# States on the partitions: a selective scan laid out by 4 states x 32 channels, its sum over the states made in four column quarters of TensorE

## The chip, the cores and the metric

The kernel runs on one core of one Trainium2 chip. The time is the device time of one execution in microseconds, as the median of several runs. Beside it there is one profiled execution, with a record of every instruction of the five engines: TensorE (PE, with its weight loads PEld), VectorE (DVE), ScalarE (ACT), GpSimd (POOL) and SyncE (SP), which here only issues DMAs.

## The reference, cut to what matters

One decoder layer on `x[8, 256, 256]` (batch, time, width) in f32: a Mamba block, a cross attention with a feed-forward, and a mixture of 160 experts. The change is in the Mamba block (512 channels, 16 states):

```python
u = silu(conv4(x @ in_x) + conv_b)                  # [256 t, 512 channels]
dt, Bm, Cm = split(u @ x_proj, [16, 16, 16])        # Bm, Cm: [256 t, 16 states]
delta = softplus(dt @ dt_proj + dt_b)               # [256 t, 512]
A = -exp(A_log)                                     # [512, 16]
for t in range(256):                                # per channel d and state n
    h[d, n] = h[d, n] * exp(delta[t, d] * A[d, n]) + delta[t, d] * u[t, d] * Bm[t, n]
    y[t, d] = sum_n h[d, n] * Cm[t, n]
y = (y + u * D_param) * silu(x @ in_z)
x = layernorm(x + y @ out_proj)
```

Then `x = layernorm(...)` of the attention block on `ctx`, with a feed-forward of 1024, and `x = layernorm(x + moe(x))` with the 8 best of 160 experts per token. The 8 batch rows are independent up to the experts.

## The kernel before, in words

**Stages.** The first stage does Mamba, attention and routing for one batch row after another (0 to some 855 us), then what is left of the last row (to some 950), then the expert blocks to the end. The change touches the first stage.

**A step.** The scan of a row is 16 steps, one for each state. Partitions are 128 channels, and the free side holds 4 channel groups x 256 times, so a step is one tile of 128 x 1024. In step n

- GpSimd makes `g = du * B[n]` (`product`, L348),
- ScalarE makes the four decays `exp(delta * A)` into PSUM (`decays`, L353),
- VectorE runs two scans of 512 columns into the PSUM tile `states` (`scans`, L363) and reads them out times `C[n]` into `h` (`read_out`, L372),
- TensorE adds `h` into the row's sum `ya` with two products against the identity (`summed`, L381); at state 0 it also adds `D_param * u` by a diagonal matrix (L384).

The rows `B[n]` and `C[n]` are the same for all channels, so they are loaded from DRAM to all partitions, four states in one DMA of 512 KB (`bc_load`, L340).

**What runs beside the steps.** Three Python generators are advanced by `go()` between the parts of a step: `head(b + 1)` makes the next row's u, z, B, C and delta (convolution L279, SiLU, Exp, L324, Ln, the subtraction on GpSimd L329, L332, `du` L334); `rest(b - 1)` does the row before: gate (L400), output projection (L406), layernorm, attention (scores' maximum L466, values L494), feed-forward (L524, L535, L540), layernorms and router (probabilities L567, the best eight L577, their sum L584, its reciprocal L592, places L602); `scatter` (L628) writes the routing table by indirect DMAs on GpSimd.

**What sets the order.** For PE, ACT, DVE and POOL the whole stage lies in one `manual_schedule`: each engine runs its instructions in the order in which the program text emits them, so the order is the sequence of `go()` calls in the loop over the 128 steps. The products run `LEAD` = 3 steps ahead of the scans:

```python
scans(b, n, made)
while ahead < min(i + LEAD + 1, len(steps)) and "du" in rows_made[steps[ahead][0]]:
    product(*steps[ahead], rows_made[steps[ahead][0]])
    ahead += 1
```

The SP queue, which issues the DMAs, is ordered by a scheduler. Two PSUM banks turn for everything but the held tiles (`decay`, `states`) and `ya`.

Of the kernel before, what the change touches and what calls it, by code (L numbers as in the profile page):

```python
# [29 lines left out]
NG = 4  # L30
# [17 lines left out]
C_BQ = C_ALOG + KI * NS  # L48
# [14 lines left out]
def decoder_layer(  # L63
# [109 lines left out]
    with ExitStack() as first:  # L173
# [3 lines left out]
        m3 = first.enter_context(tc.tile_pool(name="m3", bufs=3))  # L177
        m4 = first.enter_context(tc.tile_pool(name="m4", bufs=4))
        pools["ps"] = first.enter_context(tc.tile_pool(name="ps_front", bufs=2, space=PSUM))
# [3 lines left out]
        a2 = first.enter_context(tc.tile_pool(name="a2", bufs=2))  # L183
# [6 lines left out]

        def load_x(b):
            xt = m2.tile([P, KD, S], F32, tag="xt", name=f"xt_{b}")
            nc.sync.dma_start(xt, x_t[:, b, :].rearrange("(k p) t -> p k t", p=P))
            return xt
# [3 lines left out]
        xt0 = load_x(0)  # L198
        in_sb = weight(in_w, KD, 2 * DI, "in_sb")
# [10 lines left out]
        none = wts.tile([P, D], F32, name="none")  # L210
# [17 lines left out]
        na = wts.tile([P, KI * NS], F32, name="na")  # L228
        exps()
        nc.scalar.activation(na, cv[:, C_ALOG : C_ALOG + KI * NS], AF.Exp)  # L230
# [6 lines left out]


        decay = [held.tile([P, 2, S], F32, name=f"decay{j}") for j in range(KI // 2)]
        for t in decay:  # L240
            nc.vector.memset(t[:, :, 0:1], 0.0)
        states = held.tile([P, KI, S], F32, name="states")
        states_f = states.rearrange("p k t -> p (k t)")
# [5 lines left out]
        def head(b, xt, made):  # L249

            u = m2.tile([P, KI, S], F32, tag="u", name=f"u_{b}")
            sz = m2.tile([P, KI, S], F32, tag="sz", name=f"sz_{b}")

            def projected(j):

                pj = bank(f"pj_{b}_{j}").rearrange("p (e t) -> p e t", e=2)
                for e in range(2):
                    o = (2 * j + e) * P
                    for k in range(KD):
                        nc.tensor.matmul(  # L260
                            pj[:, e, :], in_sb[:, k, o : o + P], xt[:, k, :], start=(k == 0), stop=(k == KD - 1)
                        )
                return pj

            for j in range(KI // 2):
                pj = projected(j)
                yield
                for e in range(2):
                    k = 2 * j + e
                    nc.scalar.activation(  # L270
                        u[:, k, :], pj[:, e, :], AF.Identity, bias=cv[:, C_CONVB + k : C_CONVB + k + 1],
                        scale=cv[:, C_CONVW + (k + 1) * NTAP - 1 : C_CONVW + (k + 1) * NTAP],
                    )
                yield
                for e in range(2):
                    k = 2 * j + e
                    for i in range(NTAP - 1):
                        late = NTAP - 1 - i
                        nc.vector.scalar_tensor_tensor(  # L279
                            u[:, k, late:], pj[:, e, : S - late],  # L280
                            cv[:, C_CONVW + k * NTAP + i : C_CONVW + k * NTAP + i + 1], u[:, k, late:], ALU.mult, ALU.add,
                        )
                    if e == 0:
                        yield
            for j in range(KI // 2):
                pz = projected(KI // 2 + j)
                yield
                nc.scalar.copy(sz[:, 2 * j : 2 * j + 2, :], pz)
            nc.scalar.activation(u, u, AF.Silu)
# [6 lines left out]
            xd = m2.tile([RK + 2 * NS, S], F32, tag="xd", name=f"xd_{b}")  # L296
            nc.scalar.copy(xd, px[: RK + 2 * NS, :S])
            bc_d = dr.tile([2, NS, S], F32, tag="bc_d", name=f"bc_d_{b}")
            nc.sync.dma_start(bc_d.rearrange("a n t -> (a n) t"), xd[RK:, :])
            made["bc_d"] = bc_d  # L300
# [5 lines left out]
            delta = m2.tile([P, KI, S], F32, tag="delta", name=f"delta_{b}")  # L306
# [26 lines left out]
            du = m2.tile([P, KI, S], F32, tag="du", name=f"du_{b}")  # L333
            nc.gpsimd.tensor_mul(du, delta, u)  # L334
            made.update(u=u, sz=sz, delta=delta, du=du)

        def bc_load(b, i, n, bc_d):

            t = m2.tile([P, NG, S], F32, tag=f"bc{i}", name=f"bc{i}_{b}_{n}")
            nc.sync.dma_start(t, bc_d[i, n : n + NG, :].partition_broadcast(P))  # L340
            return t

        def product(b, n, made):

            if n % NG == 0:
                made["b_rows"] = bc_load(b, 0, n, made["bc_d"])
            g = m4.tile([P, KI, S], F32, tag="g", name=f"g_{b}_{n}")
            nc.gpsimd.tensor_mul(g, made["du"], mid(made["b_rows"][:, n % NG, :], KI))  # L348
            made[n] = g.rearrange("p k t -> p (k t)")

        def decays(b, n, made):
            for k in range(KI):
                nc.scalar.activation(  # L353
                    decay[k // 2][:, k % 2, 1:], made["delta"][:, k, 1:], AF.Exp,
                    scale=na[:, k * NS + n : k * NS + n + 1],
                )

        def scans(b, n, made):

            gf = made.pop(n)  # L360
            for j in range(KI // 2):
                part = slice(j * NT, (j + 1) * NT)
                nc.vector.tensor_tensor_scan(  # L363
                    states_f[:, part], decay[j].rearrange("p k t -> p (k t)"), gf[:, part], 0.0, ALU.mult, ALU.add
                )

        def read_out(b, n, made):

            if n % NG == 0:
                made["c_rows"] = bc_load(b, 1, n, made["bc_d"])  # L370
            h = m3.tile([P, KI, S], F32, tag="h", name=f"h_{b}_{n}")
            nc.vector.tensor_mul(h, states, mid(made["c_rows"][:, n % NG, :], KI))  # L372
            made["h"] = h.rearrange("p k t -> p (k t)")

        def summed(b, n, made, hf):

            if n == 0:
                made["ya"] = [acc.tile([P, NT], F32, tag="acc", name=f"ya_{b}_{j}") for j in range(KI // 2)]
            ya, u = made["ya"], made["u"]
            for j in range(KI // 2):  # L380
                nc.tensor.matmul(ya[j], ident, hf[:, j * NT : (j + 1) * NT], start=(n == 0), stop=(n == NS - 1))  # L381
            if n == 0:
                for k in range(KI):
                    nc.tensor.matmul(  # L384
                        ya[k // 2][:, (k % 2) * S : (k % 2 + 1) * S], diag[:, k, :], u[:, k, :],
                        start=False, stop=False,
                    )

        def rest(b, sz, ya):

            xn = a2.tile([P, TT, D], F32, tag="xn", name=f"xn_{b}")
            nc.sync.dma_start(xn, x[b].rearrange("(c p) d -> p c d", p=P))
            ct = a2.tile([P, KD, S], F32, tag="ct", name=f"ct_{b}")
            nc.sync.dma_start(ct, cx_t[:, b, :].rearrange("(k p) t -> p k t", p=P))
            cn = a2.tile([P, TT, D], F32, tag="cn", name=f"cn_{b}")
            nc.sync.dma_start(cn, cx[b].rearrange("(c p) d -> p c d", p=P))

# [24 lines left out]
            def biased(pp, bias, name):  # L422
                dst = a1.tile([P, KD, S], F32, tag=name, name=f"{name}_{b}")
# [7 lines left out]
            kt = biased(pk, C_BK, "kt")  # L431
            x1 = a2.tile([P, TT, D], F32, tag="x1", name=f"x1_{b}")
            layernorm(x1, xn, f"x1_{b}")
            yield
            val = a1.tile([P, TT, D], F32, tag="val", name=f"val_{b}")
# [14 lines left out]
            qt = biased(pq, C_BQ, "qt")  # L450
# [18 lines left out]
            prob = a1.tile([P, TT, S], F32, tag="prob", name=f"prob_{b}")  # L469
# [176 lines left out]
        with tc.manual_schedule(engines={E_.PE, E_.Activation, E_.DVE, E_.Pool}):  # L646
            for _ in head(0, xt0, rows_made[0]):
# [12 lines left out]
            steps = [(b, n) for b in range(B) for n in range(NS)]  # L660
            ahead = 0
            for i, (b, n) in enumerate(steps):
                made = rows_made[b]
                if n == 0:
                    if b + 1 < B:
                        heads.append(head(b + 1, load_x(b + 1), rows_made[b + 1]))
                    if b == 0:
                        product(0, 0, made)
                        ahead = 1
                        decays(0, 0, made)  # L670
                if n == NS - 2:
                    while heads:
                        go(heads)
                scans(b, n, made)
                while ahead < min(i + LEAD + 1, len(steps)) and "du" in rows_made[steps[ahead][0]]:
# [4 lines left out]
                go(rests)  # L680

                if i > 0:
                    b0, n0 = steps[i - 1]
                    summed(b0, n0, rows_made[b0], rows_made[b0]["h"])
                if n % 2 == 0:
                    go(heads)
                read_out(b, n, made)
                if n == 0 and b > 0:
                    before = rows_made[b - 1]
                    rests.append(rest(b - 1, before["sz"], before["ya"]))  # L690
                    next(rests[-1])
                else:
                    go(rests)
                go(heads)
                go(scattered)
                if len(rests) > 1:
                    go(rests)
                if len(rests) > 1 and n > 0:
                    go(rests)
# [6 lines left out]
            summed(B - 1, NS - 1, made, made["h"])  # L706
# [239 lines left out]
def laid_out(inputs):  # L946
# [5 lines left out]
    def columns(v, width=1):  # L952
# [13 lines left out]
        "in_w": get(a + "in_proj_w").T,  # L966
# [13 lines left out]
                columns(get(a + "A_log"), NS),  # L980
# [34 lines left out]
```

## Time and profile before

| | before |
|---|---|
| median of 3 runs | 1525.78 us (1523.56 to 1527.69) |
| profiled execution, its own time | 1523.81 us |
| its span | 1522.1 us |
| mean granted TensorE clock | 0.872 |
| busy: PE / PEld | 1125.7 / 747.6 us |
| busy: DVE / ACT / POOL | 875.8 / 667.5 / 882.7 us |
| scan stage, first scan to the end of the last row's steps | 44 to some 855 us |

How to read it: busy time is a sum over the whole span, and the stages differ. In the scan stage all four compute engines are busy by turns, in the expert stage (950 to 1522 us) GpSimd and TensorE are. PEld is the loading of weights into TensorE, which runs beside its products. An f32 product is recorded as two passes. A number in brackets behind an instruction is the idle time of its engine ahead of it, and the arrow names what ended it.

### The profile page before, as it was taken

What the parts mean: (1) busy time and instruction counts of PE and PEld (TensorE: products, weight loads), DVE (VectorE), ACT (ScalarE), POOL (GpSimd) and SP (SyncE); (2) the same over time, 40 slices, a digit from 0 to 9 for tenths busy, and PEclk for the clock granted to TensorE, in tenths of its full rate; (3) what the DMA queues carried; (4) which work ended last, traced back from release to release, by engine and by line L of the source; (5) the groups of instructions that cost most, each with busy time, mean ns of one, the idle gap of its engine ahead of it and who ended that gap; (6) DMA issues with size and microseconds to landing.
All of it is one profiled execution on the core that took longest, in us unless ns stands there. A gap on an engine that the chain in (4) does not pass through costs nothing. (4 is left out here: it accounts for less than half of the span.)

```text
span 1522.1 us, 16364 instructions
## 1 busy us (share of the span) xinstructions
PE 1125.7 (74%) x4319; PEld 747.6 (49%) x4319; DVE 875.8 (58%) x1773; ACT 667.5 (44%) x1540; POOL 882.7 (58%) x713
## 2 busy tenths in 40 slices
PE   4567688787888878877788661088888888868675
PEld 3324455455455545554455441065666666644333
DVE  2789679669777787787688218189333333310000
ACT  4375654845855757648545331022222222212222
POOL 1664365664756756847676015565666666637775
PEclk8779998889989989989889775589999999986877
DMA  8212812121212313134211000077867778634443
GB/s 274 72 47 87 295 34 67 46 62 50 50 49 57 44 47 77 42 55 44 62 29 14 21 7 8 7 226 206 245 189 215 218 228 249 191 107 134 132 135 90
DMA packets 110294, 160.20 MB, mean 105 GB/s; under 512 B 20756, under 2 KB 77622, under 8 KB 110192
## 3 DMA queue, kind: packets, MB, share of 16 engines
q1 hardware_dynamic: 77680, 114.50, 27.1%
q0 software_dynamic: 20704, 33.81, 8.3%
q10 hardware_dynamic: 11808, 10.75, 2.0%
q8 instruction: 38, 0.62, 0.2%
q14 instruction: 64, 0.52, 0.2%
HBM read 152.15 MB, written 43.58 MB: 129 GB/s over the span
## 5 line engine op out<-in xcount | busy, mean ns | idle before, releaser
L348 POOL TENSOR_TENSOR g<-du,bc 128x1024 f32<-128x1024 f32 x128 | 299.9, 2354 | 87.4 <-DVE states L363 69.9
L363 DVE TENSOR_TENSOR_SCAN states<-decay,g 128x512 f32<-128x512 f32 x256 | 314.6, 1229 | 58.7 <-ACT decay L353 25.9
L353 ACT ACTIVATE decay<-delta,na 128x255 f32<-128x255 f32 x512 | 238.0, 474 | 130.1 <-DVE states L363 119.2
L830 POOL DMA_INDIRECT xg<-x_d,tokens x216 | 216.0, 1000 | 131.6 <-PE bt L841 121.9
L381 PE MATMUL ya<-h,ident 128*128 128x512 f32 x512 | 264.0, 648 | 29.9 <-DVE h L372 29.9
L843 DVE COPY bx<-bt 128x256 f32<-128x256 f32 x216 | 91.5, 424 | 180.6 <-PE bt L841 179.6
L852 PE MATMUL by<-we,bg 128*128 128x256 f32 x432 | 151.3, 432 | 44.5 <-ACT bg L850 36.8
L381 PEld LDWEIGHTS ya<-h,ident 128*128 128x128 f32 x512 | 102.3, 208 | 135.2 <-issue 78.7
L850 ACT ACTIVATE bg<-bh 128x128 f32<-128x128 f32 x216 | 59.8, 277 | 247.7 <-PE bh L846 243.2
L372 DVE TENSOR_TENSOR h<-states,bc 128x1024 f32<-128x1024 f32 x128 | 156.2, 1220 | 7.9
L628 POOL DMA_INDIRECT tab_d<-pair_no,placei x128 | 130.7, 1021 | 42.0 <-issue 30.0
L934 POOL DMA_INDIRECT y<-y_d,sloti x128 | 121.0, 945 | 58.4 <-issue 35.3
L940 PE MATMUL yn<-y,diags 128*128 128x256 f32 x256 | 110.8, 551 | 42.4 <-DMA y<-y_d,sloti 41.3
L846 PEld LDWEIGHTS bh<-bx,we 128*128 128x128 f32 x864 | 130.0, 193 | 20.2 <-DVE bx L843 8.2
L846 PE MATMUL bh<-bx,we 128*128 128x128 f32 x864 | 134.7, 279 | 4.1 <-DVE bx L843 2.8
L852 PEld LDWEIGHTS by<-we,bg 128*128 128x128 f32 x432 | 65.2, 189 | 96.7 <-ACT bg L850 96.2
L940 PEld LDWEIGHTS yn<-y,diags 128*128 128x128 f32 x256 | 56.2, 257 | 94.8 <-DMA y<-y_d,sloti 90.0
L941 DVE TENSOR_TENSOR xs<-xs,yn 128x512 f32<-128x512 f32 x8 | 5.5, 688 | 158.1 <-PE yn L940 158.1
L524 PE MATMUL ph<-x2t,w_sb 128*128 128x256 f32 x256 | 71.9, 443 | 31.6 <-ACT x2t L512 31.2
L841 PE MATMUL bt<-ident,xg 128*128 128x128 f32 x432 | 83.5, 275 | 3.8 <-DMA xg<-x_d,tokens 3.8
L524 PEld LDWEIGHTS ph<-x2t,w_sb 128*128 128x128 f32 x256 | 56.3, 225 | 51.3 <-ACT x2t L512 37.0
L260 PE MATMUL pj<-xt,in_sb 128*128 128x256 f32 x256 | 65.7, 403 | 17.6 <-DMA in_sb<-in_in_w_dram 8.3
(220 smaller groups left out, 1609.9 us busy)
## 6 DMA issues: line engine op xcount, KB each, us to landing
we<-in_experts_dram SPq DMA_DIRECT2D x216, 256.0 KB, 3.4
bc<-bc_d SPq DMA_DIRECT2D x64, 512.0 KB, 5.7
y_d<-bo SPq DMA_DIRECT2D x216, 128.0 KB, 3.0
y_d<-none ACTq DMA_DIRECT2D x1, 9216.0 KB, 31.4
xg<-x_d,tokens POOLq DMA_INDIRECT x216, 3.6
xt<-in_x_t_dram SPq DMA_DIRECT2D x8, 256.0 KB
w_sb<-in_w_dram SPq DMA_DIRECT2D x2, 1024.0 KB, 10.9
xn<-in_x_dram SPq DMA_DIRECT2D x8, 256.0 KB, 5.2
```

Of the source, the lines that this page charges most:

```text
L348: nc.gpsimd.tensor_mul(g, made["du"], mid(made["b_rows"][:, n % NG, :], KI))
L353: nc.scalar.activation(decay[k // 2][:, k % 2, 1:], made["delta"][:, k, 1:], AF.Exp, scale=na[:, k * NS + n : k * NS + n + 1],)
L363: nc.vector.tensor_tensor_scan(states_f[:, part], decay[j].rearrange("p k t -> p (k t)"), gf[:, part], 0.0, ALU.mult, ALU.add)
L372: nc.vector.tensor_mul(h, states, mid(made["c_rows"][:, n % NG, :], KI))
L381: nc.tensor.matmul(ya[j], ident, hf[:, j * NT : (j + 1) * NT], start=(n == 0), stop=(n == NS - 1))
L524: nc.tensor.matmul(ph[:, i, :], w1_sb[:, k, f * P : (f + 1) * P], x2t[:, k, :], start=(k == 0), stop=(k == KD - 1),)
L628: nc.gpsimd.indirect_dma_start(out=tab_views[i * TOPK + j], out_offset=bass.IndirectOffsetOnAxis(ap=placei[:, c, j : j + 1], axis=0), in_= ...
L830: nc.gpsimd.indirect_dma_start(out=xg[i % LANES], out_offset=None, in_=x3_d, in_offset=bass.IndirectOffsetOnAxis(ap=tokens[:, i : i + 1], ...
L846: nc.tensor.matmul(ph, w[:, k * P : (k + 1) * P], xt[:, k * P : (k + 1) * P], start=(k == 0), stop=(k == KD - 1))
L852: nc.tensor.matmul(py, g, w[:, KD * P :], start=True, stop=True)
L934: nc.gpsimd.indirect_dma_start(out=y8[:, j, :], out_offset=None, in_=y_d, in_offset=bass.IndirectOffsetOnAxis(ap=sloti[:, i, j : j + 1], a ...
L940: nc.tensor.matmul(pn[:, c, :], diags[:, i, j, :], y8[:, j, :], start=False, stop=(j == TOPK - 1))
```

## The change

A step is now 32 channels with all 16 states, in place of one state with all 512 channels. The partitions are 4 states x 32 channels, the free side 4 groups of states x 256 times. There are still 16 steps to a row (`NC` = 16 channel groups), with a tile of 128 x 1024 in each, and the product, the four decays, the two scans and the read-out keep their number, shapes and engines.

- **The sum over the states** now runs over the partitions too. A matrix `over` of 128 x 32 adds the four states of each channel. Every four steps, `summed` makes 16 products of 256 columns, each into 32 partitions of `ya`: the four steps of a group go to the four quarters of the partitions, named by `tile_position`. The part `D_param * u` goes first (`skipped`, at step 2).
- **B and C** of a row are loaded once, into two tiles of 128 x 1024 (`rows_of`: eight DMAs of 128 KB, each to 32 partitions).
- **delta and delta * u** need each channel on four partitions. Both are stored to DRAM at the end of a head (`spread_d`, 512 KB each) and loaded back for two steps at a time (`spread`: eight DMAs of 64 KB), up to four pairs ahead (`PAIRS`).
- **The order**: heads start at step 2 of a row in place of step 0, advance twice a step in place of one and a half times, and are flushed at step 10 in place of 14. `rest` gets one more stage ahead of the gate, and its later stages are reached at other points of the steps.
- **Buffers**: `in_w` comes as two halves; `xt`, `u`, `v`, `delta`, `xd` and the tiles of `rest` have one buffer; kt, qt, values and probabilities share one tile (`early`) with `ht`; `none` shares one with `pr`; `h` has five buffers; the spread tiles have four.

```diff
-NG = 4
+NR = 4
+NG = NS // NR
+CH = P // NR
+NC = DI // CH
+NP = NC // 2
+PAIRS = 4
 LEAD = 3
...
+        over = wts.tile([P, CH], F32, name="over")
+        nc.vector.tensor_add(over, ident[:, :CH], ident[:, CH : 2 * CH])
+        for r in range(2, NR):
+            nc.vector.tensor_add(over, over, ident[:, r * CH : (r + 1) * CH])
...
-            du = m2.tile([P, KI, S], F32, tag="du", name=f"du_{b}")
-            nc.gpsimd.tensor_mul(du, delta, u)
-            made.update(u=u, sz=sz, delta=delta, du=du)
-
-        def bc_load(b, i, n, bc_d):
-
-            t = m2.tile([P, NG, S], F32, tag=f"bc{i}", name=f"bc{i}_{b}_{n}")
-            nc.sync.dma_start(t, bc_d[i, n : n + NG, :].partition_broadcast(P))
-            return t
+            spread_d = dr.tile([2, DI, S], F32, tag="spread_d", name=f"spread_d_{b}")
+            nc.sync.dma_start(spread_d[0].rearrange("(k p) t -> p k t", p=P), delta)
+            nc.gpsimd.tensor_mul(v, delta, u)
+            nc.sync.dma_start(spread_d[1].rearrange("(k p) t -> p k t", p=P), v)
+            made.update(u=u, sz=sz, spread_d=spread_d, spread=[])
+
+        def rows_of(b, a, made):
+
+            for r in range(NR):
+                nc.sync.dma_start(
+                    made["bc"][a][r * CH : (r + 1) * CH],
+                    made["bc_d"][a].rearrange("(g r) t -> r g t", r=NR)[r].partition_broadcast(CH),
+                )
+
+        def spread(b, j, made):
+
+            both = []
+            for a, name in enumerate(("spread_delta", "spread_du")):
+                t = m3.tile([P, 2, S], F32, tag=name, name=f"{name}_{b}_{j}")
+                for r in range(NR):
+                    nc.sync.dma_start(
+                        t[r * CH : (r + 1) * CH],
+                        made["spread_d"][a, 2 * j * CH : 2 * (j + 1) * CH, :].rearrange("(q i) t -> i q t", i=CH),
+                    )
+                both.append(t)
+            made["spread"].append(both)
...
-            nc.gpsimd.tensor_mul(g, made["du"], mid(made["b_rows"][:, n % NG, :], KI))
+            nc.gpsimd.tensor_mul(g, made["bc"][0], mid(made["spread"][n // 2][1][:, n % 2, :], NG))
...
-                nc.tensor.matmul(ya[j], ident, hf[:, j * NT : (j + 1) * NT], start=(n == 0), stop=(n == NS - 1))
+            hs = [made.pop(("h", k * NR + q)) for q in range(NR)]
+            for g in range(NG):
+                for q in range(NR):
+                    nc.tensor.matmul(
+                        made["ya"][k // 2][q * CH : (q + 1) * CH, (k % 2) * S : (k % 2 + 1) * S], over, hs[q][:, g, :],
+                        start=False, stop=(g == NG - 1), skip_group_check=True, tile_position=(0, q * CH),
+                    )
...
+                if n == 2:
+                    skipped(b, made)
+                    if b + 1 < B:
+                        heads.append(head(b + 1, rows_made[b + 1]))
+                if n % NR == 0 and i > 0:
                     b0, n0 = steps[i - 1]
-                    summed(b0, n0, rows_made[b0], rows_made[b0]["h"])
-                if n % 2 == 0:
-                    go(heads)
+                    summed(b0, n0 // NR, rows_made[b0])
+                go(heads)
                 read_out(b, n, made)
...
+                if n == NC - 6:
+                    while heads:
+                        go(heads)
```

The changed kernel is longer, so a line has another number in it. The ones that the prediction uses, before and after: product L348 and L378, decays L353 and L384, scans L363 and L393, read-out L372 and L400, sums L381 and L418, scores' maximum L466 and L502, softplus L324 and L339, L332 and L347, feed-forward's sum L540 and L576, the two GpSimd products behind its layernorm L543/L544 and L579/L580, layernorm statistics L143 and L148, the best eight L577 and L613, the reciprocal L592 and L628.

## The prediction

> **What bounds the kernel now.** The page first. It gives the shares of the whole span and the costliest groups; the three lines below are TensorE's sums of the states, VectorE's scans and the header.
>
> ```profile
> span 1522.1 us, 16364 instructions
> ...
> L363 DVE TENSOR_TENSOR_SCAN states<-decay,g 128x512 f32<-128x512 f32 x256 | 314.6, 1229 | 58.7 <-ACT decay L353 25.9
> ...
> L381 PE MATMUL ya<-h,ident 128*128 128x512 f32 x512 | 264.0, 648 | 29.9 <-DVE h L372 29.9
> ```
>
> The sums are issued 256 times (two per step, 128 steps) and recorded 512 times: an f32 product is two passes, each with its own weight load. No engine is full over the span, so the second view is the busy times in one stretch. VectorE's timeline repeats itself every 102.5 us in the scan stage (the maximum over the scores, L466, starts at 488.08 and at 590.56); this row is one such round, sixteen steps.
>
> ```profile
> 487.90:590.40 102.50, 83.78 (x285) 54.63 (x284) 81.08 (x115) 66.56 (x143) 67.48 (x44) 0.92 0.29 52
> ```
>
> TensorE is busy 84 us, VectorE 81 (85 with the tenth of a microsecond after each instruction), ScalarE and GpSimd 67. Four in-order queues that hand work to each other set the round, so the third view is VectorE's own timeline of the round: what it waits for, in brackets.
>
> ```profile
> 491.65 2.57 DVE L363 TENSOR_TENSOR_SCAN states<-decay,g 128x512 f32<-128x512 f32 x2 [2.88 <-ACT decay L353]
> ...
> 512.08 1.22 DVE L332 SCALAR_TENSOR_TENSOR delta<-v,delta 128x1024 f32<-128x1024 f32 x1 [0.96 <-POOL delta L329]
> ...
> 517.21 2.56 DVE L363 TENSOR_TENSOR_SCAN states<-decay,g 128x512 f32<-128x512 f32 x2
> 519.87 1.23 DVE L372 TENSOR_TENSOR h<-states,bc 128x1024 f32<-128x1024 f32 x1
> 521.22 2.56 DVE L363 TENSOR_TENSOR_SCAN states<-decay,g 128x512 f32<-128x512 f32 x2
> ...
> 527.55 2.56 DVE L363 TENSOR_TENSOR_SCAN states<-decay,g 128x512 f32<-128x512 f32 x2 [2.44 <-POOL g L348]
> 532.62 0.69 DVE L540 TENSOR_TENSOR x<-x,pf 128x512 f32<-128x512 f32 x1 [2.50 <-PE pf L535]
> ...
> 554.30 0.33 DVE L577 MAX8 best<-pr 128x8 f32<-128x160 f32 x1 [3.87 <-ACT pr L567]
> ...
> 590.56 0.69 DVE L466 TENSOR_REDUCE top<-psc 128x2 f32<-128x512 f32 x1 [2.96 <-PE psc L459]
> ```
>
> An undisturbed step is 4.0 us (517.21 to 521.22). The six waits shown are 15.6 us; five small ones (pm 0.85, decay 0.31, 0.24 and 0.20, pn 0.17) add 1.8: 17.4 of 102.5. So VectorE's work, 85.1 us, is the floor, and the change is worth what it does to 17.4 us. TensorE is 18 us short of full; its relief counts only in waits that end on it. The last views are TensorE's, ScalarE's, GpSimd's and the DMA issues.
>
> ```profile
> 525.51 7.07 PE L535 MATMUL pf<-w_sb,ht 128*128 128x256 f32 x32
> ...
> 586.91 1.88 PE L381 MATMUL ya<-h,ident 128*128 128x512 f32 x4
> 588.63 1.89 PE L459 MATMUL psc<-kt,qt 128*128 128x256 f32 x8
> ```
> ```profile
> 502.22 1.15 ACT L321 ACTIVATE delta<-e,ones 128x1024 f32<-128x1024 f32 x1
> ...
> 554.29 1.28 ACT L133 ACT_TABLE_LOAD   x1
> ```
> ```profile
> 520.36 2.35 POOL L334 TENSOR_TENSOR du<-delta,u 128x1024 f32<-128x1024 f32 x1
> ...
> 536.54 1.27 POOL L543 TENSOR_TENSOR x<-x,rv 128x512 f32<-128x512 f32 x1 [2.12 <-ACT x L157]
> ```
> ```profile
> cn<-in_cx_dram SPq DMA_DIRECT2D x8, 256.0 KB, 2.6
> x_d<-x SPq DMA_DIRECT2D x8, 256.0 KB, 4.3
> ```
>
> **Edits at no price.** Product, four decays, two scans and read-out keep engine, count, shape and element count; I keep 2354, 474, 1229 and 1220 ns. SP gets 512 spread loads, 64 row loads and 16 stores for the 64 row loads of before; the 8 small stores stay. At the 0.37 to 0.47 us that its issue rows show, 592 issues are 220 to 280 us of an 850 us stage, and a slot of the four spread pairs is free six steps before its next use. So SP hides it, except at the turn of a batch (below), where nothing stands between store and load.
>
> **The sums.** Before: 1.72 us from start to start for each step's four passes, 27.5 a round. After: 16 products of 256 columns every four steps, 32 passes. No row shows column quarters. The upper bound is the same shape back to back, L535: 7.07 us for 32 passes, no gain. The lower is a quarter of it, 1.8. I take half, 3.7: the two passes of one product need the same quarter, so in order only the second pass of one and the first of the next can overlap. Relief: 27.5 to 14.8 us a round.
>
> The Trainium skill, page "TensorE: Matmul & The Clock Gate", section "Measured speedup vs the span model", has 2.38 times for three column tiles of 512 columns; by it the group is an estimated 3.0 us, and the sum below falls by 2 us. No run here shows it yet.
>
> **The round after.** I lay the changed queues out with the rows' durations, clock 0 at step 2's scan. Each place, after against before (from here on lines are the changed kernel's, unless a line of before is compared):
>
> Scores (L502, step 5). The query projection starts when ScalarE has copied x1t (16.65), takes 1.75; the group of sums now stands behind it, 18.4 to 22.1; psc is ready at 24.1. VectorE arrives at 23.85: 0.25 against 2.96.
>
> Step 8's decays stand behind two table loads, two SiLU and two copies, as before: 2.7 against 2.88.
>
> Softplus (L339, L347). Heads advance twice a step, and the layernorm of x2 (2.15) now stands ahead of the Exp and the +1 (2.2) in ScalarE's queue, while VectorE's L339 moves ahead of step 9's read-out. ScalarE: decays from 41.4, layernorm from 43.25, Exp and +1 to 47.6; VectorE has ended its scan at 45.0: 2.6 against nothing. Behind the wait stand h and the next scan. Then table load, Ln, GpSimd's subtraction (2.35) to 54.25, L347 ahead of h at 52.6: 1.6 against 0.96.
>
> Feed-forward (L576). No sums between its products any more: 0.9 against 2.50.
>
> Turn of the batch. GpSimd's queue: subtraction to 54.25, two gains 2.5, two scatters 2.3, a product, then v to 63.9. The store of v: 0.5 issue and 5.0 landing (512 KB; the nearest row is 256 KB in 4.3) to 69.4; four issues (1.9) and 2.6 landing to 73.8. The next batch's first product waits for this, to 76.2, and behind it in GpSimd's queue stand L579 and L580 (2.55), which VectorE's statistics of step 14 need: 78.8. VectorE arrives at 74.9: 3.9 against nothing. Product 14's wait of 2.44 goes. For the landings the bounds are 2.6 and 5.7 (the 512 KB row load), a stall of 1.5 to 7.7.
>
> The same skill, page "DMA: Bandwidth & Descriptors", "Rules for kernel authors", speaks against 64 KB pieces on a quarter of the partitions (mostly overhead; take one transfer over 128). Its fit for GpSimd's path, 2.0 us plus bytes over 436 GB/s, makes the trip an estimated 7.7 us in place of 9.9, the stall 1.7, the kernel 13 us less; the rows decide here.
>
> Router (L613, L628). Best waits 2.75 against 3.87. But the reciprocal of den now stands ahead of h and waits for ScalarE's table load 1.28, decays 1.83, chosen and den 0.8: 3.9 behind the start of best, which is 2.0 long: 1.9 against nothing.
>
> Small ones: 2.3 (u 0.8, pm 0.8, decay 0.7) against 1.8. Sum 18.9 against 17.4: +1.5 a round.
>
> **The start.** Input weights in halves let the first product begin some 2.7 us sooner (8.26 us for 1 MB now). Then delta's end, 38.8 before, is 36.1; product 2.35, store 5.4, loads 4.5, first product 2.35: first scan at 50.8 against 44.2, +6.6.
>
> **Sum.** Six rounds 9; the last batch has no head and keeps the reliefs, less the reciprocal: -3.5; start 6.6; TensorE less busy gets a lower clock (0.92 at 82% busy, 0.86 at 73% between 100 and 200 us), some 5 us on 16 us of its work on the path per round. In all +17. The profiled execution took 1523.8 us (span 1522.1 and 1.7 around it), 2.0 below the median 1525.8; on the median 1543.
>
> **Rivals.** *The quarters run one after another.* Then the change does not do what it says: 7.07 a group. Scores +3.2, and at the turn the last group delays sz and the router's counts by 2.4: 5.6 a round, seven rounds 39: 1582. For: no row shows two products at once. Against: they name different quarters.
>
> *The trip through memory is short.* If v's end to landed loads is 6.1 us or less (cn's 2.6 for both landings gives 7.5), the 3.9 goes: 23 us less, 1520, 0.4% faster. Against: bc_d's 32 KB store already takes 4.6.
>
> *ScalarE runs ahead.* If TensorE's relief lets ScalarE reach the Exp 4.2 us sooner, the softplus waits go too, 25 us more: 1495. Against: its queue there holds 11 us of its own work from step 8 on, none of it waiting for a sum.
>
> **How the numbers follow.** Forecast 0.47 (1520 to 1566), serial 0.22, short trip 0.17, ahead 0.14. The range 1495 to 1590 leaves out most of the last and little else. A measurement of this kernel can tell 0.3%, 4.6 us, from no change. Faster: ahead 0.14, short trip 0.10, forecast 0.02: 0.26; same 0.11; slower 0.63.
>
> **What would show it.** 32 passes of L418 in near 3.7 us (7 serial, 1.8 all four); L502's wait near zero; waits at L339, L347, L148 and L628 of 2.6, 1.6, 3.9, 1.9; the round near 104; first scan near 51. A round under 100 would prove me wrong.

## The result

The changed kernel takes 1539.28 us (median of 4 runs, 1538.55 to 1548.54) against 1525.8: 1.0103 times the time before, interval 1.0062 to 1.0144. A second measurement on another chip gave 1.0059 (1.0035 to 1.0083). It is slower, by 13.5 and by 9 us, small but clear of the intervals; 1543 was forecast. The profiled execution took 1539.88 us, 16.1 more than that of before. From its page:

```profile
PE 996.8 (65%) x4831; PEld 698.0 (45%) x4831; DVE 878.9 (57%) x1776; ACT 667.4 (43%) x1540; POOL 882.7 (57%) x713
...
L418 PE MATMUL ya<-h,over 128*32 128x256 f32 x1024 | 88.8, 471 | 30.2 <-DVE h L400 30.2
```

TensorE lost 129 us of work (1125.7 before) and 50 of weight loads, VectorE gained 3, ScalarE and GpSimd stayed as they were, and the time went up. The busy times of one steady round, from one maximum of the scores to the next (columns as in the same view of before):

```profile
487.74:593.42 105.68, 67.81 (x350) 48.07 (x349) 81.93 (x117) 66.42 (x142) 67.42 (x44) 0.81 0.35 73
```

Before it was 102.5 with TensorE busy for 84 at a granted clock of 0.92. VectorE's waits in this round, from its timeline:

```profile
487.74 0.68 DVE L502 TENSOR_REDUCE top<-psc 128x2 f32<-128x512 f32 x1
...
498.94 2.56 DVE L393 TENSOR_TENSOR_SCAN states<-decay,g 128x512 f32<-128x512 f32 x2 [2.83 <-ACT decay L384]
502.78 0.88 DVE L538 SCALAR_TENSOR_TENSOR x<-pm,total,x 128x256 f32<-128x256 f32 x2 [1.27 <-PE pm L530]
...
511.76 1.23 DVE L339 SCALAR_TENSOR_TENSOR e<-delta,e 128x1024 f32<-128x1024 f32 x1 [2.47 <-ACT delta L336]
518.32 2.27 DVE L347 SCALAR_TENSOR_TENSOR delta<-v,delta 128x1024 f32<-128x1024 f32 x1 [1.51 <-POOL delta L344]
...
535.15 0.69 DVE L576 TENSOR_TENSOR x<-x,pf 128x512 f32<-128x512 f32 x1 [2.30 <-PE pf L571]
...
544.37 0.75 DVE L148 BATCH_NORM_STATS2 st_x<-x 128x6 f32<-128x256 f32 x2 [2.12 <-POOL x L580]
558.34 0.33 DVE L613 MAX8 best<-pr 128x8 f32<-128x160 f32 x1 [2.54 <-ACT pr L603]
...
562.11 0.17 DVE L628 RECIPROCAL den<-den 128x2 f32<-128x2 f32 x1 [1.71 <-ACT den L620]
```

The wait for the scores is gone, those for ScalarE and GpSimd stand where the prediction put them. L347 also takes 2.27 us where the same pass took 1.22 before. It starts 0.07 us behind a GpSimd product of 1.27 us (L552), and the next one on GpSimd, which starts while the pass runs, takes 2.13 us in place of 1.27:

```profile
519.59 2.13 POOL L553 TENSOR_TENSOR x<-x,rv 128x512 f32<-128x512 f32 x1
```

TensorE's timeline has the sums at their best (granted clock 1.00) and, at the turn of the row, at half clock (0.50):

```profile
482.40 1.93 PE L418 MATMUL ya<-h,over 128*32 128x256 f32 x32
484.26 1.99 PE L495 MATMUL psc<-early 128*128 128x256 f32 x8
```
```profile
553.38 1.43 PE L597 MATMUL pl<-rt_sb,x_t 128*128 128x160 f32 x4 [4.91 <-ACT x_t L593]
...
557.76 3.64 PE L418 MATMUL ya<-h,over 128*32 128x256 f32 x32
```

Thirty-two passes take 1.93 us, where full-width passes of 256 columns took 7.07. And the trip through memory, from SP's timeline and GpSimd's: the store of v is issued at 528.87, the loads of `spread_du` behind it at 535.73, when the store has landed, the row's first product at 539.43, and behind it on GpSimd stand L579 and L580, which the statistics wait for.

```profile
528.87 0.38 SPq L351 DMA_DIRECT2D spread_d<-v  x1
529.35 2.37 SPq L368 DMA_DIRECT2D spread_delta<-spread_d  x4
535.73 1.71 SPq L368 DMA_DIRECT2D spread_du<-spread_d  x4
```
```profile
539.43 2.35 POOL L378 TENSOR_TENSOR g<-bc,spread_du 128x1024 f32<-128x1024 f32 x1 [5.96 <-DMA spread_du<-spread_d]
```

**Where the 16 us lie.** A row is counted here from its first scan to the next row's first scan (the eighth to its last scan, which starts at 832 us before and 841 after):

| us | before | after | difference |
|---|---|---|---|
| up to the first scan | 44.2 | 50.4 | +6.2 |
| row 1 | 81.0 | 83.9 | +2.9 |
| rows 2 and 3 | 101.6, 108.7 | 95.5, 105.7 | -9.1 |
| rows 4 to 7 | 102.1, 102.6, 102.5, 102.4 | 108.1, 105.7, 103.5, 104.3 | +12.0 |
| row 8, to its last scan | 86.8 | 84.4 | -2.4 |
| last scan to the first routing scatter behind it | 93.2 | 90.3 | -2.9 |
| that scatter to the first fetch of an expert block | 61.8 | 72.2 | +10.4 |
| expert stage | 535.2 | 534.2 | -1.0 |

Two traces of each kernel show how far such a table can be trusted: from the first to the last scan 787.8 and 787.4 us before, 791.0 and 793.2 after. The second trace of the changed kernel has its first scan at 48.6 us, and 7.1 us in place of 10.4 in the line of the scatter.

VectorE's timeline tells what the rows differ by. In rows 4 to 7 its idle times over 0.13 us add up to 69.4 us before and 79.5 after, its work to 340.2 and 342.1: 10.1 of the 12.0 us are waits. In rows 2 and 3 the idle times fall from 45.4 to 37.0. Most of that is the wait for the attention: 3.8 and 4.7 us at the reciprocal of the sums (L476) and 6.0 and 5.2 at L502 before, none and 1.0 and 1.3 after. Before, the attention's product L484 ran in these two rows at a granted clock of 0.55 and 0.50 (3.49 and 3.78 us, 1.93 in the steady rows); after the change it takes 1.99 us in every row from the second to the seventh.

### The profile page after: what moved, and what is told of

Its sections match the earlier page's. It is cut to its first block, busy times and chain, and to the rows that moved or that the text cites. A ratio compares the mean times of both kernels' runs of the same rounds, so it can differ in the third digit from the quotient of the medians.

```text
span 1538.2 us, 18276 instructions
## 1 busy us (share of the span) xinstructions
PE 996.8 (65%) x4831; PEld 698.0 (45%) x4831; DVE 878.9 (57%) x1776; ACT 667.4 (43%) x1540; POOL 882.7 (57%) x713
## 5 line engine op out<-in xcount | busy, mean ns | idle before, releaser
L378 POOL TENSOR_TENSOR g<-bc,spread_du 128x1024 f32<-128x1024 f32 x128 | 300.3, 2355 | 118.8 <-DVE states L393 61.5
L393 DVE TENSOR_TENSOR_SCAN states<-decay,g 128x512 f32<-128x512 f32 x256 | 314.5, 1229 | 62.9 <-ACT decay L384 29.2
L384 ACT ACTIVATE decay<-spread_delta,na 128x255 f32<-128x255 f32 x512 | 238.4, 474 | 180.9 <-DVE states L393 152.7
L400 DVE TENSOR_TENSOR h<-states,bc 128x1024 f32<-128x1024 f32 x128 | 156.1, 1219 | 10.7 <-PE ya L418 5.0
L664 POOL DMA_INDIRECT tab_d<-pair_no,placei x128 | 125.8, 983 | 46.3 <-issue 29.9
L418 PE MATMUL ya<-h,over 128*32 128x256 f32 x1024 | 88.8, 471 | 30.2 <-DVE h L400 30.2
L171 PE MATMUL pt_x<-ident,x 128*128 128x128 f32 x96 | 25.5, 369 | 115.2 <-ACT x L162 102.9
L560 PEld LDWEIGHTS ph<-x2t,w_sb 128*128 128x128 f32 x256 | 59.9, 238 | 61.7 <-ACT x2t L548 50.5
L171 PEld LDWEIGHTS pt_x<-ident,x 128*128 128x128 f32 x96 | 13.5, 173 | 130.4 <-ACT x L162 115.6
```

The costliest lines, as they stand in the source:

```text
L378: nc.gpsimd.tensor_mul(g, made["bc"][0], mid(made["spread"][n // 2][1][:, n % 2, :], NG))
L384: nc.scalar.activation(decay[g // 2][:, g % 2, 1:], delta[:, n % 2, 1:], AF.Exp, scale=na[:, n * NG + g : n * NG + g + 1])
L393: nc.vector.tensor_tensor_scan(states_f[:, part], decay[j].rearrange("p g t -> p (g t)"), gf[:, part], 0.0, ALU.mult, ALU.add)
L400: nc.vector.tensor_mul(h, states, made["bc"][1])
L560: nc.tensor.matmul(ph[:, i, :], w1_sb[:, k, f * P : (f + 1) * P], x2t[:, k, :], start=(k == 0), stop=(k == KD - 1),)
L664: nc.gpsimd.indirect_dma_start(out=tab_views[i * TOPK + j], out_offset=bass.IndirectOffsetOnAxis(ap=placei[:, c, j : j + 1], axis=0), in_= ...
```

## The experiments

The runs e1 to e4, e5 to e8 and e9 to e12 shared a chip each. On those chips the kernel before takes 1555 to 1557 us, so ratios are to the kernel before on the same chip, and the stages are taken from the traces, one trace to a run. The expert stage, which no edit touches, takes 562 us there in the trace of the kernel before (535 above) and 563 to 570 in those of the new layout. So a difference of a few us in the whole time says little about an edit, and the stage says more; lines of an edited kernel are shifted by one or two, or more behind the larger edits. "Stage" is first to last scan, "behind" is last scan to first fetch.

| run | ratio to before (interval) | stage | behind |
|---|---|---|---|
| before, e9 | | 787.8, 787.4 | 155.0, 155.0 |
| after, e5 | 1.0103 (1.0062 to 1.0144), 1.0059 (1.0035 to 1.0083) | 791.0, 793.2 | 162.5, 160.3 |
| e1 wide | 1.0559 (1.0519 to 1.0599) | 868.5 | 162.0 |
| e2 by quarter | 1.0344 (1.0297 to 1.0390) | 826.8 | 166.0 |
| e3 reciprocal later | 1.0050 (1.0032 to 1.0069) | 790.1 | 158.8 |
| e4 softplus later | 1.0049 (1.0028 to 1.0070) | 786.7 | 161.2 |
| e6 stale | 1.0040 (1.0017 to 1.0063) | 787.4 | 156.9 |
| e7 warm | 1.0079 (1.0043 to 1.0114) | 780.1 | 159.3 |
| e8 all three | 1.0347 (1.0302 to 1.0393) | 821.2 | 166.3 |
| e10 best later | one run, 1619.66 us | 831.6 | 169.6 |
| e11 softplus and split | 1.0059 (1.0034 to 1.0085) | 787.1 | 163.3 |
| e12 with warm too | 1.0061 (1.0035 to 1.0086) | 777.6 | 163.7 |

The theory of the prediction: each wait of VectorE that the new order adds is a cost of its own, and the sum over a row is the change. The rivals: TensorE's quarters decide; or the row is a chain through four queues in which a wait that is taken away comes back at the next place.

### What the quarters are worth: e1 and e2

```diff
-        over = wts.tile([P, CH], F32, name="over")
...
+        over = wts.tile([P, NR, P], F32, name="over")
+        nc.vector.memset(over, 0.0)
...
-                        made["ya"][k // 2][q * CH : (q + 1) * CH, (k % 2) * S : (k % 2 + 1) * S], over, hs[q][:, g, :],
-                        start=False, stop=(g == NG - 1), skip_group_check=True, tile_position=(0, q * CH),
+                        made["ya"][k // 2][:, (k % 2) * S : (k % 2 + 1) * S], over[:, q, :], hs[q][:, g, :],
+                        start=False, stop=(g == NG - 1), skip_group_check=True,
```

> The sums of four steps with weights of 128 columns in place of 32: the matrix of each step of a group adds the four states into that step's 32 partitions and zeros into the other 96, so the 16 products go over the whole array, one after another. All else stays. A group of 32 passes should take 7.1 us at full clock in place of 1.93. Theory A (the quarters are worth what the prediction's serial rival charges, because scores and the turn of the row wait for a group): the maximum of the scores waits 3.5 us or so where it waited for nothing, the places at the turn wait 5 to 10 more, 9 to 14 us a round, 1590 to 1630 us. Theory B (TensorE stands beside the path, its relief is worth nothing): under 1545 us.

```diff
-            for g in range(NG):
-                for q in range(NR):
+            for q in range(NR):
+                for g in range(NG):
```

> The same 16 products of a group in another order: the four of one quarter one after another, then the next quarter's. Theory A (products overlap only where neighbours in the queue name different quarters): three in four neighbours now share a quarter, a group takes 6 us or more in place of 1.93, and the time goes up as with full-width sums. Theory B (each quarter takes its products on its own, whatever their order): 1.9 us and 1539 us, as the changed kernel.

A group in TensorE's timeline, first of e1, then of e2:

```profile
541.80 7.17 PE L420 MATMUL ya<-h,over 128*128 128x256 f32 x32
```
```profile
520.74 4.59 PE L418 MATMUL ya<-h,over 128*32 128x256 f32 x32
```

In both the time goes up, as theory A has it. Full width costs 75 us of the stage and the order by quarters 34 (against e5's 793.2), although TensorE is about as busy in them as before the change (1130 and 1075 us; 1126 before). Sums after every step were hidden there; in groups of four steps they are only hidden when they are short. The places of the waits came out otherwise: in e1's steady rows the scores wait 1.80 us where 3.5 were expected and the places 0.7, and three read-outs in each row wait 1.4 to 4.1 us for a buffer of `h` that a late group has yet to read. In e2 a group takes 4.59 us where 6 or more were expected, and the cost is half of that at full width, not the same.

How far the quarters run side by side depends on the order: 7.17, 4.59 and 1.93 us for the same 32 passes. The starts of the single passes show how. At full width a pass starts every 0.216 us. In the changed kernel (the group at 482.40) four passes start within 0.02 us of each other, and the next four 0.22 us or so later, eight times. In e2 the eight passes of one quarter start about 0.22 us apart, and the next quarter's begin 0.89 us after the first, with the fifth pass: three times 0.89 and 1.91 for the last quarter make 4.59.

The prediction's rival of serial quarters had 39 us for groups of 7.07. e1, whose groups are that long, costs 75: the rival left out the read-outs that wait for a buffer. e2's groups of 4.59 already cost 34.

### Single waits: e3, e4 and e6

```diff
-            nc.vector.reciprocal(den, den)
             yield
             yield
+            nc.vector.reciprocal(den, den)
```

> The reciprocal of the sum of the best eight is moved two half steps later, to just ahead of the places. Theory A (its wait for ScalarE, 1.7 us, is a cost of its own that stands ahead of the read-out in VectorE's queue): the wait goes, 1.2 to 1.7 us a round in seven rounds, 1527 to 1531 us. Theory B (the places wait for the same ScalarE work anyway): the wait moves to them, 1537 to 1540 us.

```profile
558.38 1.23 DVE L400 TENSOR_TENSOR h<-states,bc 128x1024 f32<-128x1024 f32 x1 [1.01 <-PE ya L418]
...
562.01 0.33 DVE L638 SCALAR_TENSOR_TENSOR key<-pn,chosen 128x160 f32<-128x160 f32 x1 [1.14 <-PE pn L626]
```

Theory B, as VectorE's timeline above shows: the 1.71 us are gone from the reciprocal, and 1.01 stand at the read-out, which now comes before the turn's group of sums has released its buffer of `h`, and 1.14 in place of 0.45 at the places. The stage is 790.1 us (791.0 and 793.2 without the edit), and the ratio, 1.0050 against 1.0059, cannot be told from that without it.

```diff
             yield
             yield
+            yield
             nc.vector.scalar_tensor_tensor(e, delta, 1.0, e, ALU.subtract, ALU.subtract)
```

> VectorE's two passes of the softplus stand half a step later in its queue, behind the read-out of their step in place of ahead of it, as in the kernel before. Theory A (their waits for ScalarE and GpSimd, 2.5 and 1.5 us, lie on VectorE's path): the read-out of 1.2 us fills half of the first wait, the end of the second pass does not move, 1.2 us a round, some 8 us less: 1531 us. Theory B (the path runs through ScalarE there and VectorE would only wait elsewhere): 1539 us.

```profile
509.58 2.28 DVE L340 SCALAR_TENSOR_TENSOR e<-delta,e 128x1024 f32<-128x1024 f32 x1 [1.14 <-ACT delta L336]
...
517.09 1.22 DVE L348 SCALAR_TENSOR_TENSOR delta<-v,delta 128x1024 f32<-128x1024 f32 x1 [1.43 <-POOL delta L345]
```

Theory A, by the stage: 2.47 became 1.14, the second wait stayed, and the stage is 4 to 6.5 us shorter. The slow pass has changed places: the first now takes 2.28 us and the second 1.22 (1.23 and 2.27 without the edit), and now it is the first that starts 0.07 us behind a GpSimd product of 1.26. The gain is in rows 3 to 7, together 9 us shorter than in e5; the second row is 4.7 longer. Of the whole time the comparison shows 1.0049 against 1.0059, which it cannot tell apart.

```diff
+            if b > 0:
+                t = m3.tile([P, 2, S], F32, tag="spread_du", name=f"spread_du_{b}_0")
+                for r in range(NR):
+                    nc.sync.dma_start(
+                        t[r * CH : (r + 1) * CH],
+                        rows_made[b - 1]["spread_d"][1, : 2 * CH, :].rearrange("(q i) t -> i q t", i=CH),
+                    )
+                made["first_du"] = t
...
+                if (a, j) == (1, 0) and b > 0:
+                    both.append(made["first_du"])
+                    continue
```

> Leaves the trip through memory out for one piece: the first two steps of each row but the first take delta * u from the row before, loaded ahead of the store of this row's; so the first product of a row waits for no store. Theory A (the trip is a cost of its own, by the wait of the statistics, 2.1, 4.1 and 2.1 us in three of the rows and 0.5 in a fourth): these waits go, some 9 us less than the changed kernel on the same chip. Theory B (what GpSimd gains there is waited for at the next place): within 3 us of it.

```profile
539.62 0.74 DVE L148 BATCH_NORM_STATS2 st_x<-x 128x6 f32<-128x256 f32 x2
```

Theory A, at half its size: the waits of the statistics are gone from VectorE's timeline (the line has no bracket), and the stage is 4 to 6 us shorter than the changed kernel's. The median is 4.2 us lower (1560.47 against 1564.63), nearer to theory B's bound of 3 than to 9, and nine of its ten executions lie below all ten of the changed kernel. The trip itself, 10.6 us from the end of v to the first product, is hidden for the most part.

### TensorE's clock: e7

```diff
+        zeros = wts.tile([P, CH], F32, name="zeros")
+        nc.vector.memset(zeros, 0.0)
...
             pt = turned(x3, f"x3_{b}")
+            if b + 1 < B:
+                for i in range(16):
+                    q = i % NR
+                    nc.tensor.matmul(
+                        rows_made[b + 1]["ya"][0][q * CH : (q + 1) * CH, :S], zeros, w2_sb[:, 0, :],
+                        start=False, stop=False, skip_group_check=True, tile_position=(0, q * CH),
+                    )
             yield
```

> Sixteen more products with zero weights stand in TensorE's queue between the transposes of x3 and the router's product, where TensorE now idles 4.9 us and its granted clock is 0.5; they add zeros to the row's sum. Theory A (the low clock costs time on the path: the router's product, 4.7 us for 12 passes, and the turn's group of sums, 3.64 us, run at half speed, and the best eight wait 2.5 us for them): the clock is back to 1 by then, and 2 us a round go, some 12 us less than the changed kernel on the same chip. Theory B (the low clock there costs nothing, or the products themselves delay the router): no gain, up to 10 us more.

```profile
539.05 3.64 PE L594 MATMUL ya<-w_sb,zeros 128*32 128x256 f32 x32
544.03 0.81 PE L606 MATMUL pl<-rt_sb,x_t 128*128 128x160 f32 x4 [1.34 <-ACT x_t L602]
...
546.81 3.64 PE L420 MATMUL ya<-h,over 128*32 128x256 f32 x32
```

TensorE's timeline: the router's product is at full clock (four passes in 0.81 us in place of 1.43), the best eight wait 0.6 to 2.0 us in place of 2.54, and the group of sums behind it is at half clock again. In the traced execution the stage is 11 to 13 us shorter, as theory A has it, but its expert stage is 6.6 us longer than that of e5 (570.0 and 563.4). The times do not bear a gain out: two executions took 1559 us, the traced one among them, and four 1568 to 1570, against a median of 1564.63 for the changed kernel. What the clock costs over the whole stage stays open.

### The order: e8, e10, e11 and e12

e8 is e4's edit and these two, a stage more ahead of the best eight and delta * u in two parts:

```diff
             exps()
             yield
             yield
+            yield
...
-            nc.gpsimd.tensor_mul(v, delta, u)
-            nc.sync.dma_start(spread_d[1].rearrange("(k p) t -> p k t", p=P), v)
+            for ks in (slice(0, 1), slice(1, KI)):
+                nc.gpsimd.tensor_mul(v[:, ks, :], delta[:, ks, :], u[:, ks, :])
+                nc.sync.dma_start(
+                    spread_d[1, ks.start * P : ks.stop * P, :].rearrange("(k p) t -> p k t", p=P), v[:, ks, :])
```

> Three edits to the order together: the softplus half a step later as before, the best eight half a step later, and delta * u made and stored in two parts, first the 128 channels that the next row's first steps need. Theory A (each wait of VectorE is a cost of its own): softplus 1.2 us a round, best 1.2 to 2.5, the shorter trip 2 at the start and up to 2 a round: 25 to 35 us less than the changed kernel, 10 to 20 less than the kernel before. Theory B (the row is a chain through four queues, and a wait taken away comes back at the next place): 0 to 10 us less than the changed kernel.

Both theories fell: it is 28 us of the stage longer. In its program the maximum of the scores had moved behind the scan of step 6, from behind the read-out of step 5. The best eight alone, in e10:

> Of the three edits of the run before, the best eight half a step later alone. Theory A (this edit did the harm: the extra stage of the row that is finishing holds up the next row's attention by half a step against the head of the row after, so the maximum of the scores falls into step 6): rows of 108 us or more from the third on and some 1600 us. Theory B (the harm came from the delta * u in two parts, or from all together): rows near 104 us and 1565 us or less.

Theory A: rows of 112.6 us and more from the third on, and 1619.66 us in the one execution that was measured. TensorE's timeline of one row, and VectorE's:

```profile
633.56 3.78 PE L520 MATMUL pat<-prob_t,early 128*128 128x256 f32 x8
...
639.27 3.57 PE L530 MATMUL pm<-attn_w,at 128*128 128x256 f32 x8
```
```profile
631.95 2.57 DVE L393 TENSOR_TENSOR_SCAN states<-decay,g 128x512 f32<-128x512 f32 x2 [4.05 <-ACT decay L384]
642.95 0.88 DVE L538 SCALAR_TENSOR_TENSOR x<-pm,total,x 128x256 f32<-128x256 f32 x2 [7.17 <-PE pm L530]
```

The best eight belong to the row that is finishing. A stage more there holds up the next row's attention by half a step, because `go()` serves the older row first; the head does not move. The products of the attention then run at half clock (3.78 and 3.57 us for eight passes; 1.99 in the changed kernel), and VectorE waits 7.17 us for what cost 1.27. Their neighbours do too: from 626.93 to 642.84 TensorE is busy without a break at a granted clock of 0.51, on work that takes some 8.5 us in the changed kernel's round. That is about what a row is longer by (8 us), but no run held the order and changed the clock alone. The kernel before has such a row too, its third, of 108.7 and 108.6 us in its two traces; TensorE's timeline there:

```profile
282.78 3.78 PE L484 MATMUL pat<-prob_t,val 128*128 128x256 f32 x8 [1.17 <-ACT prob_t L480]
```

> The other two edits together: softplus half a step later, delta * u made and stored in two parts. Theory A (each takes away a wait of its own): the softplus 6.5 us of the scan stage as before, the shorter trip up to 1.5 us a row and 0.5 at the start: some 12 us of the stage less than the changed kernel's 793 us, and about the time of the kernel before. Theory B (the trip's waits are covered as far as they can be): the softplus alone, 787 us.

Theory B: 787.1, no less than the softplus edit alone (786.7). At the start the first scan comes at 50.1, and at 49.4 in e8, which has the same split: within what the runs with the unsplit trip show (48.4 to 52.5).

> The same two edits and the sixteen products with zero weights that keep TensorE at work ahead of the router. Theory A (the stage's 13 us of the run with these products hold and add up): a stage of 770 to 775 us, 10 us less than the kernel before. Theory B (they were the chance of one execution: its other executions were 9 us longer): within 3 us of the run without them.

The stage is nearer to theory A, 777.6 us where 770 to 775 were expected, 10 less than the kernel before and 9.5 less than e11's. The whole does not gain: the median is e11's (1567.84 and 1567.57), with ten executions from 1556.03 to 1570.75, the traced one at 1562.38. The gain of the stage is shown for the traced execution alone. No version beats the kernel before.

### Behind the last scan: e5 and e9

> The changed kernel as it is, on the chip of the next three, for what the routing table's scatter costs behind the last scan. Theory A (its waits are a property of the changed kernel): the first fetch of the expert blocks is again some 162 us behind the last scan, where the kernel before has 155, and the ratio to the kernel before is again near 1.010. Theory B (chance of one execution): 155 us or less, and a ratio nearer 1.006.

> The kernel before as it is, for a second trace of it. Theory A (the change lengthens what follows the last scan): 155 us again from the last scan to the first fetch of the expert blocks, where seven traces with the new layout have 157 to 166; and the rows again take 101.6, 108.7 and then 102 to 103 us. Theory B (155 was chance): 158 us or more.

e5 is split: 160.3 us behind the last scan, near theory A, but a ratio of 1.0059, which is theory B's. e9 is theory A's, 155.0 us and rows of 101.4, 108.6 and then 102.1 to 102.5. Before, the time from the first of these scatters to the fetch of the table is 52.8 us in both traces, in the twelve traces of the new layout 57.9 to 63.0, with an unchanged list of instructions. GpSimd's timeline of the changed kernel, where the two kernels part:

```profile
958.60 0.96 POOL L664 DMA_INDIRECT tab_d<-pair_no,placei  x1 [9.46 <-DMA tab_d<-pair_no,placei]
```

Before, the longest wait for an earlier scatter to land is 1.9 us (2.4 in e9); with the new layout the longest is 4.6 to 9.7 us, 24 to 30 us into the list, and the table's fetch waits 7.7 to 10.5 us in place of 6.0 and 6.1. No other transfer runs by then (DMA share 0.00 from 950 to 960). The scatter that GpSimd waits for here was issued at 938.25 and lands at 958.3. Why it lands later than before is open: no run changed the scatter.

## Why the prediction was right, and where it was not

The sign and most waits came out. That the total came within 4 us (1539.28 against 1543, +16.1 against +17 in the profiled execution) is in part luck: 10.4 of the 16.1 us lie where the prediction had nothing, and its six rounds and its clock were too dear by about as much.

- **The start**: +6.6 forecast, +6.2 measured (+4.4 in the second trace).
- **The waits in the round** (forecast, measured): L339 2.6, 2.47; L347 1.6, 1.51; step 8's decays 2.7, 2.83; best 2.75, 2.54; the reciprocal 1.9, 1.71; scores 0.25, none. Laying four in-order queues out by the durations of the trace before gave these to 0.25 us.
- **The turn of the row**: 10.6 us measured from the end of v to the first product, 9.9 forecast (6.9 for the store and 3.7 for the loads, where 5.5 and 4.4 were forecast); but the wait behind it came in some rows only, 2.1, 4.1, 2.1 and 0.5 us and none in two, where 3.9 was summed in each. e6 puts it at 4 to 6 us in all. The estimated 7.7 us by the fit of the Trainium skill (page "DMA: Bandwidth & Descriptors", section "Anatomy of one DMA — SWDGE (gpsimd) path") was too short for this trip. The 512 loads of 64 KB landed in 2.0 and 1.9 us (medians).
- **The group of sums**: mis-sized, 3.7 forecast, 1.93 measured, next to the lower bound of 1.8. The step that failed is "only the second pass of one and the first of the next can overlap": four passes, one of each quarter, start together. The Trainium skill's rate (page "TensorE: Matmul & The Clock Gate", section "Measured speedup vs the span model") gave an estimated 3.0 us; the measured ratio of full-width to quarter passes in these runs is 7.17 over 1.93, 3.7. It was worth little in time: the forecast had charged the scores 0.25 us for the longer group.
- **Small waits**: feed-forward 1.0 to 2.3 in place of 0.9, and 4.2 to 4.7 in all for values, decays, convolution and places in place of 2.3. They about make up for the statistics: 19.6 us in this round, 18.0 in the next, 18.9 forecast.
- **Six rounds, +9**: rows 2 to 7 are +2.9. The failed step is one round for all: the third row before was 6 us longer than the steady ones, and the second row became 6 us shorter, largely by waits for the attention, whose product ran at about half clock in these rows before and at full clock after. No run separated the clock from the order. The four steady rows show +12.0, 3.0 a row, where waits and clock were to make 1.5 and about 0.8; 2.5 of the 3.0 are waits.
- **VectorE's durations**: kept in the forecast, but L347 takes 2.27 us in rows 3 to 7 in place of 1.23, a term that was put at nothing. Where this pass starts just behind a GpSimd product it is longer by about what is left of that product: 1.05 us beside 1.27, and 3.35 us in all beside a `g` of 2.35, as in rows 1 and 2 before. Shorter passes elsewhere give half of it back.
- **The clock, +5**: the granted clock fell (0.92 to 0.81 in a round), but no run separated its price. The prediction had it only as a loss; in rows 2 and 3 the attention's product ran faster than before.
- **The last row, -3.5**: -2.4 in it (-0.2 in the second trace), and -2.9 behind it (-1.7).
- **Missed altogether**: +10.4 between the last scatters and the expert blocks. Without it the kernel would have been 6 us slower in the profiled execution, in the lower part of the forecast. This largest term has no known cause.
- **Rivals**: the quarters do not run serially; e1 shows that this rival would have cost 75 us in place of its 39. The trip is not short (the 4.6 us of the 32 KB store that was set against it is the middle of only two landings, 1.5 and 7.7), and ScalarE does not run ahead at the softplus.

## What to carry to other kernels

Relief on an engine is worth what waits for it: here 129 us of TensorE's work went and 3 us were added to a steady row, because VectorE waited for ScalarE and GpSimd. Column quarters of TensorE ran side by side in full when successive products named different quarters, and the order of the loops decides that (1.93 against 4.59 us). In an order of several in-order queues, half a step can cost more (38 us in e10) than all the waits that it was to remove; move a stage only after reading which other stages move with it.

## What the runs showed of the hardware that was not expected

- 32 f32 passes of 256 columns with 32 output columns each take 1.93 us in four quarters taken in turn, 60 ns a pass, 4.59 us when four products of a quarter follow one another, 7.17 us at full width.
- In e7 a stretch of products that keeps TensorE busy for 3.64 us at half clock (granted 0.52) was followed by products near full clock (0.85, from 544.0 to 546.8), and those from 546.8 on were at half again (0.50), though TensorE had not paused.
- The same 32 scatters hold GpSimd up for 4.6 to 9.7 us at one place in all twelve traces of the new layout and for at most 2.4 us in both of the old, with nothing else on the DMA engines.
- A VectorE pass of 1.23 us takes 2.27 where it starts 0.07 us behind a GpSimd product of 1.27, and 3.35 behind one of 2.35, and the GpSimd product that starts meanwhile takes 2.13 in place of 1.27.
